# Rows of an edge's destination: from one-hot products against node tiles to a load of 32 nodes by register, and padded weights for 32 experts

## The chip, the cores and the metric

The kernel runs on one core of a Trainium2 chip. The metric is the device time of one execution in microseconds (us); three runs of the kernel before gave 5314.71, 5327.92 and 5352.43, so its median is 5327.92. The engines' names are those of the profile: PE (TensorE), DVE (VectorE), ACT (ScalarE), POOL (GpSimd), SP (SyncE, which issues DMAs here). PEld is PE's loading of weights, that is of the operand that stays in the array during a product.

## The reference

The program is a graph network of four layers, each followed by a mixture of experts. There are 3125 nodes with 256 features, and 50,000 edges with a source, a destination, 64 attributes and a weight; edges are sorted by destination. Cut to what the change touches:

```
# layer 1, messages                       row = source, col = destination
edge_in = concat([h[row], h[col], edge_attr])
msg = relu(edge_in @ W1.T + b1) @ W2.T + b2
agg = segment_sum(msg, row)               # then a GRU cell on agg and h

# layer 1, experts: 32 of 256 -> 64 -> 256, each node goes to its best one
idx = argmax(x @ router_w.T + router_b)
out = relu(relu(x @ W1[idx] + b1[idx]) @ W2[idx] + b2[idx])

# layer 2, hyperbolic convolution         c = 1
x_src, x_dst = x[src], x[dst]
msg = logmap(x_src, x_dst, c)             # needs x_src . x_dst, |x_src|^2, |x_dst|^2
```

The weighted messages of layer 2 are then summed by destination, and a mixture of 8 experts with products of 256 x 512 to 512 x 256 follows. Layer 0 is graph attention with 8 experts, layer 3 two more convolutions with 16 experts.

## The kernel before, in words

Nodes lie in 25 tiles of 128 (the last is padded), edges in 392 tiles of 128 (padded with edges to a node that is none), worked in 28 groups of `GF = 14` edge tiles. Since edges are sorted by destination, the destinations of one edge tile fall into few node tiles. `WIN[i]` lists those that tile `i` may hit, with four standard deviations to spare: 552 pairs in all, 1.41 per edge tile. At the start `windows()` (L684) tests on the chip that the data keeps within them, and a flag chooses between the branch told of here and a general one.

**Rows of the destination.** Layers 1 and 2 need, for every edge, a row that belongs to its destination: in layer 1 the product of the destination's features with a part of W1 (`q`), in layer 2 the features with their square (257 columns). Both are had by a product with a one-hot matrix. `dst_hot` (L352) loads a group's destinations as an int32 row broadcast to 128 partitions (`w_row`, 128 x 1792), and for each node tile that the group may hit it compares them with the node numbers of the partitions (`w_hot`, bf16, on DVE). To keep float32's precision, the rows are split into three bf16 parts that add up (`split3`, or by hand in layer 1). One edge tile then takes three bf16 products for each of its node tiles: 552 x 3 = 1656 products in each layer. `dst_hot` also serves the attention layer.

**Layer 1, first loop** (`mpnn_buckets`, L1169; "MQ" below). `prepare` works on up to four node tiles at a time (seven times): it collects the results of the experts before, normalises, transposes, and takes the product with W1's part; the three parts stay in SBUF (`q_parts`, name `mq_q`). It is called from the loop over groups when a group two further on needs its nodes. For each edge tile PE adds the product of 64 attributes with W1's last part (f32, in two matmul instructions) and the one-hot products in PSUM (`mq_pe`); ACT copies two tiles at a time to `mq_r` (three buffers of a group); POOL scatters every tile's rows by an indirect DMA (L570) into `slot_r`, sorted by the source. A second loop ("mb") takes the sums and the GRU from there.

**32 experts** (`moe_top1`, L1285, by `sparse_experts`, L583). Nodes are sorted into chunks of 128 of the same expert (43 chunks always, more if needed). For a chunk, `load(i)` reads the expert's weights by a register (`se_w`, 4 buffers, 128 x 385 f32) and the chunk's rows (`se_r`), which PE transposes. Products: hidden (128 rows, 64 columns of weights), ACT's relu into `se_h`, to the output (65 rows: 64 hidden ones and a row of ones for the bias, which a DVE memset sets). Loads run two chunks ahead. The rows go back by POOL's indirect DMA.

**Layer 2** (`hyper_bn`, L1537; "HB" below). For each group POOL gathers the sources' rows (`hb_r`), the one-hot matrices are made, and the node tiles that come into reach are split into parts (`hb_parts`, 4 buffers). For each edge tile PE takes the rows of the destinations (`hb_pc`), DVE multiplies and sums them with the sources' rows and copies the squares; then a chain of small operations on the group gives a factor for each edge (`hbe_` names); and with one group's delay, `sums` makes a weighted one-hot matrix (`hb_eq`, DVE) and adds up the messages by destination (`hb_acc`, f32). After every step `between()` lets a piece of other work in: chains of node work, and the products of the mixture for blocks of four node tiles that are complete, at a pace of 0.44 pieces for each call (`PACE`). The weights of these products come through SP (`hb_w`).

The order on every engine is that of the program. SP issues in order the loads of `w_row`, `mq_ea`, `se_w`, `se_r`, `hb_w` and the stores.

The lines that follow are `between`, which sets the order of the work in HB:

```
def between():
    slot[0] += 1
    step(chains)
    if products and slot[0] * PACE >= done[0] + 1:
        done[0] += 1
        step(products)
```

## Time and profile before

The profiled execution took 5317.6 us; its span is 5315.8 us, and the mean granted clock of PE 0.848 of full speed. Busy time over the span: PE 4261.4 us (80%), PEld 2837.0, DVE 2560.1 (48%), POOL 2243.8 (42%), ACT 1177.9 (22%).

| stage | from, to (us) | PE busy | DVE busy | POOL busy | clock | DMA share |
|---|---|---|---|---|---|---|
| attention and windows | 0 to 78 | 36.9 | 51.5 | 14.3 | 0.90 | 0.48 |
| GAT | 78 to 605 | 374.3 | 366.2 | 396.4 | 0.82 | 0.64 |
| 8 experts | 740 to 867 | 117.5 | 100.4 | 66.3 | 0.98 | 0.77 |
| layer 1, first loop (MQ) | 865 to 1456 | 538.4 | 117.6 | 396.7 | 0.89 | 0.52 |
| layer 1, second loop, GRU | 1458 to 2130 | 627.5 | 356.5 | 0 | 0.99 | 0.28 |
| 32 experts | 2130 to 2409 | 162.9 | 128.9 | 66.0 | 0.53 | 0.34 |
| layer 2 (HB) | 2409 to 3705 | 1151.7 | 840.9 | 386.1 | 0.92 | 0.32 |
| layer 3, convolutions | 3709 to 4848 | 896.3 | 368.6 | 748.3 | 0.80 | 0.32 |
| 16 experts | 4860 to 5315 | 313.2 | 167.3 | 120.1 | 0.79 | 0.47 |

"Busy" is the time in which the engine executes; issuing a DMA and the handling of registers are not in it. The clock is the share of full speed that the throttle granted to PE, as a mean over the stage. In a group of the profile, `out<-in` names the tiles, `128*64 128x256` is the size of the operand that stays and of the one that streams through (partitions x elements), `xN` the number of instructions, and behind the bar stand the busy time in us, the mean of one in ns, and the engine's idle time before the group with what ended most of it.

### The profile page before, as it was taken

How to read it: one execution, taken by the hardware profiler on the slowest of the kernel's cores; microseconds unless marked ns; L12 is line 12 of the kernel's file. 1: busy time of each engine (PE TensorE's matmuls, PEld its weight loads, DVE VectorE, ACT ScalarE, POOL GpSimd, SP SyncE). 2: the span in 40 equal slices, each digit the busy share in tenths (PEclk: the TensorE clock that was granted, in tenths of full speed). 3: DMA queues.
4: the chain of work that ended last, by engine and by line, in shares of the span. 5: the costliest groups of instructions: out<-in, count | busy, mean ns of one | idle time of the engine just before them, and what ended most of it. 6: DMA issues, size and time to landing. Idle time of an engine off the chain costs nothing. (4 is left out here: it accounts for less than half of the span.)

```text
span 5315.8 us, 59675 instructions
## 1 busy us (share of the span) xinstructions
PE 4261.4 (80%) x19370; PEld 2837.0 (53%) x19370; DVE 2560.1 (48%) x9525; ACT 1177.9 (22%) x2364; POOL 2243.8 (42%) x2372
## 2 busy tenths in 40 slices
PE   4687558999899999485899999988788788885694
PEld 3566446455466666343566666655445344443583
DVE  5676646211055554447766776752333313336224
ACT  2010112222233333012332443453000200002121
POOL 4777454577700000225533333200777447771521
PEclk7888778799999999557999999988898768885797
DMA  6855256455533221154333333213333223330464
GB/s 200 267 160 160 87 187 212 152 170 162 163 105 97 92 90 53 58 161 136 105 105 97 95 111 110 79 44 91 104 105 104 72 77 104 105 104 29 169 215 135
DMA packets 342776, 647.60 MB, mean 122 GB/s; under 512 B 56019, under 2 KB 248630, under 8 KB 338102
## 3 DMA queue, kind: packets, MB, share of 16 engines
q1 hardware_dynamic: 224160, 339.16, 20.5%
q0 software_dynamic: 108480, 298.44, 18.3%
q10 hardware_dynamic: 9814, 6.03, 0.4%
q8 instruction: 163, 2.67, 0.2%
q14 instruction: 159, 1.30, 0.1%
HBM read 512.20 MB, written 131.23 MB: 121 GB/s over the span
## 5 line engine op out<-in xcount | busy, mean ns | idle before, releaser
L253 POOL DMA_INDIRECT hc_wm<-hc_tabc,src_col x784 | 748.3, 954 | 658.5 <-DMA a_L_gnn_c_b_col<-in_L_gnn_c_b_col 311.8
L337 PE MATMUL w_acc<-hc_wm,w_eq 128*128 128x256 f32 x2208 | 750.5, 467 | 203.1 <-DMA hc_wm<-hc_tabc,src_col 138.4
L337 PEld LDWEIGHTS w_acc<-hc_wm,w_eq 128*128 128x128 f32 x2208 | 438.4, 223 | 515.2 <-DVE w_eq L330 235.3
L330 DVE TENSOR_SCALAR w_eq<-iota,dloc,ew 128x128 f32<-128x128 f32 (+1 forms) x784 | 300.1, 385 | 752.8 <-PE w_acc L337 745.5
L253 POOL DMA_INDIRECT hb_r<-hy_x,src_col x392 | 386.1, 985 | 640.9 <-PE hb_acc L1896 390.6
L570 POOL DMA_INDIRECT slot_x<-xn,sl_i x125 | 122.1, 977 | 969.4 <-DMA se_w<-in_L_ffn_lanes 752.4
L570 POOL DMA_INDIRECT slot_r<-mq_r,bk_i x392 | 397.0, 1013 | 196.4 <-issue 89.8
L253 POOL DMA_INDIRECT gw_m<-gat_h,src_col x392 | 404.3, 1031 | 131.9 <-issue 119.2
L1095 PE MATMUL gw_acc<-gw_m,gw_eqt 128*128 128x264 f32 x1104 | 307.3, 438 | 129.1 <-issue 89.7
L1926 PE MATMUL hb_pc<-hb_parts,w_hot 128*128 128x257 bf16 x1656 | 269.3, 294 | 135.4 <-DVE hbe_a L1931 85.6
L1095 PEld LDWEIGHTS gw_acc<-gw_m,gw_eqt 128*128 128x128 f32 x1104 | 232.6, 217 | 190.5 <-issue 94.1
L570 POOL DMA_INDIRECT rows_y<-se_y,se_to x175 | 179.6, 1026 | 350.7 <-DVE se_y L654 186.4
L1220 PE MATMUL mq_pe<-a_L_gnn_W1T_c,mq_ea 64*128 64x256 f32 x784 | 292.6, 456 | 26.7 <-ACT mq_r L1222 13.7
L1896 PE MATMUL hb_acc<-hb_r,hb_eq 128*128 128x257 f32 x1104 | 292.8, 391 | 12.9 <-DVE hb_eq L1891 12.4
L1926 PEld LDWEIGHTS <-w_hot 128*128 128x128 bf16 x1656 | 159.4, 103 | 261.4 <-DVE hbe_a L1931 124.0
L373 PEld LDWEIGHTS <-w_hot 128*128 128x128 bf16 x3312 | 182.9, 99 | 192.9 <-issue 155.6
L373 PE MATMUL mq_pe<-mq_q,w_hot 128*128 128x256 bf16 x1656 | 265.0, 288 | 0.4 <-DVE mq_q L1202 0.4
L1797 ACT ACTIVATE hb_h<-hb_ph,hb_o,hb_s 128x512 f32<-128x512 f32 (+1 forms) x224 | 162.6, 729 | 412.1 <-PE hb_ph L1795 412.0
L1896 PEld LDWEIGHTS hb_acc<-hb_r,hb_eq 128*128 128x128 f32 x1104 | 201.4, 195 | 76.9 <-issue 27.7
L648 PE MATMUL se_py<-se_w,se_h 128*128 128x256 f32 (+1 forms) x886 | 236.3, 412 | 1.3 <-ACT se_h L641 1.2
L639 PE MATMUL se_ph<-se_xT,se_w 128*128 128x256 f32 (+1 forms) x972 | 235.1, 392 | 0.6 <-DVE se_xT L622 0.5
L641 ACT ACTIVATE se_h<-se_ph,se_w 128x256 f32<-128x256 f32 (+1 forms) x243 | 110.1, 454 | 550.3 <-PE se_ph L639 373.8
(524 smaller groups left out, 7279.9 us busy)
## 6 DMA issues: line engine op xcount, KB each, us to landing
w_row<-in_dst_row SPq DMA_DIRECT2D x84, 896.0 KB
mb_r<-slot_r SPq DMA_DIRECT2D x48, 1156.5 KB
se_w<-in_L_ffn_lanes SPq DMA_DIRECT2D x34, 1026.0 KB
hb_w<-in_L_ffn_W SPq DMA_DIRECT2D x112, 256.0 KB
se_r<-slot_x SPq DMA_DIRECT2D x66, 257.0 KB
se_w<-in_L_ffn_lanes SPq DMA_DIRECT2D x32, 513.0 KB
hb_w<-in_L_ffn_Wo SPq DMA_DIRECT2D x56, 256.0 KB
mq_ea<-in_edge_attrT SPq DMA_DIRECT2D x28, 448.0 KB
```

The lines of the kernel that those rows point to most:

```text
L253: nc.gpsimd.indirect_dma_start(out=dst, out_offset=None, in_=table, in_offset=bass.IndirectOffsetOnAxis(ap=idx, axis=0))
L330: V.tensor_scalar(eq[:, :n], iota256[:, :n], dloc[:, i:i + 1], scale[:, u:u + 1], op0=OP.is_equal, op1=OP.mult)
L337: PE.matmul(acc[t][:, :width], eq[:, k * P:(k + 1) * P], m[:, u, :width], start=i == W_FIRST[t], stop=i == W_LAST[t])
L373: PE.matmul(o, hot[t][:, u * P:(u + 1) * P], parts[:, t, k, :width], start=start and j == 0, stop=j == len(ops) - 1)
L570: d = nc.gpsimd.indirect_dma_start(out=table, in_=rows, in_offset=None, out_offset=bass.IndirectOffsetOnAxis(ap=idx, axis=0)).ins
L639: PE.matmul(ph[:fp], w[:, c * f + j * P:c * f + j * P + fp], xT[:, c], start=c == 0, stop=c == 1)
L648: PE.matmul(py[:, u], h[:kp, j, u * P:(u + 1) * P], w[:kp, o2 + j * D:o2 + (j + 1) * D], start=j == 0, stop=j == nj - 1)
L1095: PE.matmul(acc[t][:, :W], eq[:, k * P:(k + 1) * P], m[:, u], start=False, stop=i == W_LAST[t])
L1220: PE.matmul(pt[:, v], ea[:, (u + v) * P:(u + v + 1) * P], w1c, start=True, stop=False)
L1797: S.activation(o[:, j, :n], ph[:, :n], AF.Relu, bias=shift[i][:, e, j:j + 1], scale=scale[i][:, e, j:j + 1])
L1896: PE.matmul(acc[t][:, :D + 1], eq[:, k * P:(k + 1) * P], b[:, u], start=i == W_FIRST[t], stop=i == W_LAST[t])
L1926: PE.matmul(pc[:, :D + 1], hot[t][:, u * P:(u + 1) * P], parts[t][:, 0, k], start=z == 0, stop=z == len(ops) - 1)
```

## The change

It has three parts.

**Destinations' rows.** In MQ and HB `near_rows` takes the place of `dst_hot` and `from_dst` (the attention layer keeps `dst_hot`). Two neighbouring edge tiles, 256 edges, have destinations within 32 nodes; `windows()` tests this too and writes a table `near_row` of each destination's distance to the first of its pair. The three parts of every node lie in a DRAM table as neighbouring rows (`q_tab`, `parts_tab`), so 32 nodes are 96 rows, which one DMA loads from an address that a register holds (`n_near`, one for each pair of edge tiles, seven in a group). `n_hot` compares the distances (a broadcast row on 96 partitions) with `third`, the number of the partition's node, 0 to 31, each three times. One product of 96 rows for an edge tile gives the sum of the parts: 392 products in each layer.

**Tables.** `prepare` writes the parts to a tile of its own and SP stores it to `q_tab`; in HB `split_to` splits the node tiles in order, up to two groups ahead, and SP stores each to `parts_tab`. `prepare` is called when a group one further on needs its nodes and the 32 rows behind them.

**32 experts.** The weights are laid out as 128 x 2 x 193 and loaded into the end of rows of 257 whose first 64 columns were set to zero once for each of four buffers. Both products are then 128 by 128; the bias of the output comes from a hidden row that is always one, and the memset for each chunk goes.

```diff
+NEAR = 32
+W_TO = [max(WIN[(g + 1) * GF - 1]) + 2 for g in range(ET // GF)]
...
+    def near_rows(pool, g, table, width, bufs=2):
+        row = pool.tile([3 * NEAR, GF * P], BF16, name="n_row")
+        nc.sync.dma_start(row, near_row[g:g + 1].to_broadcast([3 * NEAR, GF * P]))
+        hot = pool.tile([3 * NEAR, GF * P], BF16, name="n_hot")
+        V.tensor_scalar(hot, row, third, None, op0=OP.is_equal)
+        near = pool.tile([3 * NEAR, GF // 2, width], BF16, name="n_near", bufs=bufs)
+        for k in range(GF // 2):
+            i = g * GF + 2 * k
+            with tc.issue_after(near_last[0].ins) if near_last else nullcontext():
+                n = nc.values_load(col["dst"][0:1, i:i + 1], engines=[mybir.EngineType.SP], min_val=0, max_val=N)
+            near_last[:] = [nc.sync.dma_start(near[:, k], table[bass.ds(n * 3, 3 * NEAR)])]
+        return hot, near
...
+                padded = [wp.tile([P, 2, 2 * P + 1], F32, name=f"se_w{k}") for k in range(4 if f < P else 0)]
+                for w in padded:
+                    V.memset(w[:, :, :P - f], 0.0)
...
+                    if f < P:
+                        w = padded[i % 4]
+                        last = nc.sync.dma_start(w[:, :, P - f:],
+                                                 I[name][bass.ds(e * P, P)].rearrange("p (c x) -> p c x", c=2))
...
-                        if f < P:
-                            V.memset(h[f:f + 1], 1.0)
...
-                                PE.matmul(ph[:fp], w[:, c * f + j * P:c * f + j * P + fp], xT[:, c],
-                                          start=c == 0, stop=c == 1)
-                            S.activation(h[:fp, j], ph[:fp], act, bias=w[:fp, o1 + j:o1 + j + 1])
+                                PE.matmul(ph, w[:, c, :P] if f < P else w[:, c * f + j * P:c * f + (j + 1) * P],
+                                          xT[:, c], start=c == 0, stop=c == 1)
+                            bias = w[:, 0, 2 * P:] if f < P else w[:, o1 + j:o1 + j + 1]
+                            S.activation(h[:, j], ph, act, bias=bias)
...
+    near_row = tc.dram_tile([ET // GF, GF * P], BF16, name="near_row")
+    third = const.tile([3 * NEAR, 1], F32, name="third")
...
+        nc.scalar.dma_start(dr, I["dst_row"].rearrange("(a b) -> a b", b=2 * c))
+        V.tensor_copy(rr, dr)
...
+        V.tensor_copy(rb, rr)
+        nc.scalar.dma_start(near_row.rearrange("g (a b) -> (g a) b", b=2 * P), rb.rearrange("n (a b) -> n a b", b=2 * P))
...
-            q_parts = p.tile([P, NT, 3, D], BF16, name="mq_q")
+            q_tab = tc.dram_tile([NR * 3, D], BF16, name="mq_q")
...
-                    o = q_parts[:, t0 + t:t0 + t + m]
+                    o = tp.tile([P, 2, 3, D], BF16, name="mq_o", bufs=2)[:, :m]
...
+                    nc.sync.dma_start(q_tab.rearrange("(t p k) d -> p t k d", p=P, k=3)[:, t0 + t:t0 + t + m], o)
...
-                    ahead = WIN[min((g + 2) * GF, ET) - 1][-1]
-                    while blocks and blocks[0][0] <= ahead * P:
+                    ahead = W_TO[min(g + 1, ET // GF - 1)]
+                    while blocks and blocks[0][0] < ahead * P:
...
-                    hot = dst_hot(ep, g)
+                    hot, near = near_rows(ep, g, q_tab, D, 3)
...
-                            from_dst(pt[:, v], hot, i, q_parts, D, start=False)
+                            PE.matmul(pt[:, v], hot[:, (u + v) * P:(u + v + 1) * P], near[:, u // 2], start=False, stop=True)
...
+            def split_to(end):
+                while split[0] < end:
+                    t = split[0]
+                    split[0] += 1
+                    o = wp.tile([P, 1, 3, D + 1], BF16, name="hb_parts", bufs=2)
+                    split3(sp, o[:, :, :, :D], xn[:, t:t + 1])
+                    split3(sp, o[:, :, :, D:], x2[:, t:t + 1].unsqueeze(2))
+                    nc.sync.dma_start(parts_tab[3 * t * P:3 * (t + 1) * P].rearrange("(p k) d -> p k d", k=3), o[:, 0])
...
-                hot = dst_hot(ep, g, 1)
-                for t in sorted(hot):
-                    if t not in parts:
-                        parts[t] = wp.tile([P, 1, 3, D + 1], BF16, name="hb_parts", bufs=4)
...
+                split_to(min(NT, W_TO[min(g + 2, ET // GF) - 1]))
+                hot, near = near_rows(ep, g, parts_tab, D + 1, 3)
...
-                    ops = [(t, k) for t in WIN[i] for k in range(3)]
-                    for z, (t, k) in enumerate(ops):
-                        PE.matmul(pc[:, :D + 1], hot[t][:, u * P:(u + 1) * P], parts[t][:, 0, k],
-                                  start=z == 0, stop=z == len(ops) - 1)
+                    PE.matmul(pc[:, :D + 1], hot[:, u * P:(u + 1) * P], near[:, u // 2], start=True, stop=True)
```

## The prediction

> **What bounds the kernel now.** I read the page's 40 slices first, one slice being 133 us:
>
> ```profile
> PE   4687558999899999485899999988788788885694
> DVE  5676646211055554447766776752333313336224
> POOL 4777454577700000225533333200777447771521
> PEclk7888778799999999557999999988898768885797
> ```
>
> No one engine carries the span. The change touches three stretches: the first loop of the message layer ("MQ", 865 to 1456 us, slices 7 to 11), the 32 experts (2244 to 2370, slices 17 and 18, clock 5) and the hyperbolic layer ("HB", 2409 to 3705, slices 19 to 28). The groups name their work:
>
> ```profile
> L570 POOL DMA_INDIRECT slot_r<-mq_r,bk_i x392 | 397.0, 1013 | 196.4 <-issue 89.8
> L1926 PE MATMUL hb_pc<-hb_parts,w_hot 128*128 128x257 bf16 x1656 | 269.3, 294 | 135.4 <-DVE hbe_a L1931 85.6
> L1220 PE MATMUL mq_pe<-a_L_gnn_W1T_c,mq_ea 64*128 64x256 f32 x784 | 292.6, 456 | 26.7 <-ACT mq_r L1222 13.7
> L373 PE MATMUL mq_pe<-mq_q,w_hot 128*128 128x256 bf16 x1656 | 265.0, 288 | 0.4 <-DVE mq_q L1202 0.4
> ```
>
> The change takes 1264 of each 1656 bf16 products away. What that is worth depends on who ends last in each stretch. In MQ it is POOL, by its waits between 893 and 1456:
>
> ```profile
> POOL slot_r L570 <- issue: 89.8, 295, 0.3
> POOL slot_r L570 <- ACT mq_r L1222: 53.9, 30, 10.3
> POOL slot_r L570 <- DMA slot_r<-mq_r,bk_i: 20.4, 62, 1.8
> ```
>
> A scatter is 0.97 us of work and 0.30 of issue, so 392 take 500 us at best; the stretch takes 562. PE's answers (mq_r) cost 53.9 of the difference. So a faster PE can win at most some 54 us here. The stretches say where:
>
> ```profile
> 984.00:1036.00 52.00, 51.98 (x150) 23.24 (x150) 4.90 (x12) 7.88 (x14) 30.10 (x31) 0.50 0.38 125
> 1059.00:1105.00 46.00, 46.00 (x249) 24.81 (x248) 5.21 (x7) 10.55 (x18) 35.50 (x35) 1.00 0.59 191
> 2310.00:2330.00 20.00, 20.00 (x60) 11.11 (x60) 8.86 (x29) 2.53 (x7) 6.79 (x7) 0.50 0.52 162
> 2460.00:2510.00 50.00, 37.95 (x204) 24.47 (x202) 43.70 (x268) 7.22 (x12) 38.42 (x39) 0.86 0.46 138
> 2700.00:3460.00 760.00, 719.08 (x3233) 481.08 (x3233) 526.91 (x2868) 293.88 (x550) 235.28 (x238) 0.97 0.32 99
> ```
>
> (Columns: length, busy PE, weight loads, DVE, ACT, POOL, granted clock, DMA share, GB/s.) PE is busy without a gap in the first three, yet at clock 0.50 in two of them. Rows 4 and 5: HB's start is DVE's (43.7 of 50), its long middle PE's (719 of 760).
>
> **MQ, part by part.** PE's timeline prices one edge tile:
>
> ```profile
> 1027.08 1.46 PE L373 MATMUL mq_pe<-mq_q,w_hot 128*128 128x256 bf16 x6
> 1028.47 1.22 PE L1220 MATMUL mq_pe<-a_L_gnn_W1T_c,mq_ea 64*128 64x256 f32 x2
> 1181.02 0.70 PE L1220 MATMUL mq_pe<-a_L_gnn_W1T_c,mq_ea 64*128 64x256 f32 x2
> 1181.65 0.50 PE L373 MATMUL mq_pe<-mq_q,w_hot 128*128 128x256 bf16 x3
> ```
>
> From start to start, at clock 1.0 the f32 pair takes 0.63 us and three bf16 products 0.43 (six: 0.76), so one is 0.43 − 2 × 0.11 = 0.21 and a tile after the change 0.84. At 0.50 the pair takes 1.15, six take 1.39, three 0.76, so one 0.32: a tile 1.47. POOL's pace is 1.275. **The clock therefore decides the sign:** at 1.0 POOL stays the bound and nearly all of the 54 is won; at 0.50 PE becomes the bound.
>
> What grants the clock? I weighed each product by streamed columns times rows over 128 and read the clock from one 3.4 us stretch to the next over the whole trace. From 1.0 it fell in every stretch under 600 columns per us, in 40 of 50 between 600 and 840, in 2 of 33 at 960 to 1080, and never above. From 0.50 it never rose under 720, rose in 26 of 74 between 840 and 960, and nearly always above 1020. Before the change a tile is 1024 × 64/128 + 4.22 × 256 = 1592, over 1.275 us 1250 per us: it holds. After it, 512 + 256 × 96/128 = 704: 552 per us at POOL's pace, 838 back to back at 1.0, 479 at 0.50. So the clock falls and stays down, except around the seven `prepare` blocks, whose 128-row f32 products lift it for some 10 us each.
>
> [...]
>
> Sum of MQ: 392 × 1.47 = 576; PE's share of `prepare` 57 (busy PE of 524 without the tiles' time); bursts at 1.0 save 7 × 8 tiles × 0.63 = 35. New on the path is what follows each `prepare`: the parts no longer stay in SBUF but go through SP to a DRAM table, and the next rows wait for that store. That is a copy chain, a store and a load of some 2.5 us each (transfers that size here), with 15 to 30 PE instructions between in the program's order: 3 to 4 us shown, seven times, 25. Together 623 against 562: **+60**. Bounds: −45 (clock kept, stores hidden), +110 (no bursts, 8 us at each block).
>
> SP: a load by register costs about 1.13 us (four expert weights in 3.74 us), so seven per group take 8 of the group's 18 us in MQ and of 40 in HB. Covered; bounds 0 to +60, the latter in the third rival. The row broadcast shrinks (896 KB of int32 over 128 partitions to 344 KB); the DMA share of 0.5 leaves that without effect.
>
> **HB.** In the middle there are 257 edge tiles in 760 us, 2.96 each. hb_pc holds PE 173.7 us for 1101 there, 0.158 each; 4.28 per tile become one, so PE gives back 3.28 × 0.158 = 0.52 of 2.96 us. Next late is DVE: 526.9/257 = 2.05 busy per tile, less a little (40 w_hot of 0.82 us become 18 n_hot). PE's 2.44 remains above it, but DVE already waits for PE's answers (hb_pc 74 us, hb_acc 59) and the two hand work back and forth, so I count 0.35, not 0.52: 257 × 0.35 = 90. The start (2460 to 2610) is DVE's; there the clock will fall (1448 + 193 columns per tile in 2.1 us is 780 per us), and PE at 0.50 needs 1.5 us of DVE's 2.0: nothing, −15 to +20. The last 245 us hold products alone and stay. Splitting the parts moves earlier and through SP; its DVE and ACT work is the same. **HB −90**, bounds −135 (all of 0.52) and −35 (a quarter, if DVE's chain sets the pace).
>
> **Experts.** A chunk takes 2.765 us with PE full at 0.50. Padding to 128 raises the weighted work from 512 + 1024 + 520 = 2056 to 512 + 1024 + 1024 = 2560, from 744 to 924 columns per us, into the band where the clock rose in a third of the stretches; with 35 stretches it should rise, and then hold (2560 per 1.95 us is 1310). PE would need 1.4; next late are the weights: four buffers, the next load issued when a chunk's last product frees one, then two issues (0.84) and a landing near 2 us inside 1.5 chunks, so 1.9 to 2.0 per chunk. 43 × 0.8 = 34: **−33**; without the flip 0 to +5 (64 more columns of weights to load, beside matmuls). The 43 memsets go (0.17 us, off the path).
>
> **The rest.** `windows` gains a load, ten small DVE operations and a store at the kernel's start; the first group of each layer now waits for split, store and load in series. By such latencies here (2.5 us each) +12, bounds +5 and +25.
>
> Sum: 60 − 90 − 33 + 12 = −51, from 5317.6 (span 5315.8 and 1.8 outside; the median shown, 5327.9, lies 0.2% above): **5267 us**.
>
> **Rivals.** (1) *The clock holds in MQ.* For: `prepare` lifts it, back to back 838 is only just short. Against: 552 at POOL's pace. −40 − 100 − 33 + 12: 5157. (2) *DVE takes over HB's middle.* For: 526.9 of 760 busy and 85.6 us of PE idle before hb_pc on hbe_a. Against: DVE's own waits for PE sum to 170 us. +60 − 35 − 33 + 12: 5322. (3) *Rows come late,* the slower side: one SP queue carries stores, register loads and HB's product weights in order, a store waits for the near loads issued before it, and the rows for the store. It decides where PE is the bound and reaches a group within the 8 us of its seven loads. Seven blocks of MQ at 8 us instead of 3.5 and half of HB's 28 groups at 5 us: +31 + 70 over the forecast, and no bursts at full clock, +35: 5403. Against: in HB's middle rows are issued 140 PE instructions ahead.
>
> **Numbers.** This kernel's measurement tells about 1% from no change. Forecast 0.42 (its own range 5217 to 5317: MQ and HB 25 either way each), rival (1) 0.14, (2) 0.26, (3) 0.18. Faster by over 1% (under 5264): half of the forecast, (1) and a little of (2), 0.38. Within: the other half and most of (2), 0.37. Slower: (3) and some of (2), 0.25. Range: (1)'s time to (3)'s, cut by a tenth on each side, 5150 to 5400.
>
> **What would show it.** Right: MQ at clock 0.5 to 0.7 with PE full, tiles of 1.47 us, POOL waiting for mq_r; the experts at 1.0 and 2 us a chunk; HB's middle 2.6 us per tile. Wrong: a clock of 1.0 in MQ (the weighing by rows fails), PE idle on n_near (rows late), or HB's tile pace unchanged with DVE full.

## The result

The changed kernel takes 5330.69 us (median of 12 runs, 5302.06 to 5338.44), the kernel before in the same comparison 5327.58 (12 runs, 5308.93 to 5352.43). The ratio is 0.9995, 95% interval 0.9975 to 1.0016: no change that can be measured, where 5267 us had been forecast. The profiled execution after took 5330.3 us, 12.7 more than the one before. The stages did move, against each other:

| from, to | before (us) | after (us) | difference | forecast |
|---|---|---|---|---|
| start to MQ's first scatter | 893.9 | 900.6 | +6.7 | |
| MQ, first to last scatter | 561.4 | 652.8 | +91.4 | +60 |
| second loop, GRU, to the experts' first product | 792.4 | 793.1 | +0.6 | |
| 32 experts, to the last rows out | 123.1 | 92.5 | -30.6 | -33 |
| to HB's first edge tile | 63.5 | 69.3 | +5.7 | |
| HB's edge tiles | 1033.3 | 972.2 | -61.1 | -90 |
| rest | 1848.0 | 1848.0 | 0.0 | |

The three lines without a forecast of their own were one term together, +12, and came to +13.0. (The times of the table are starts of instructions in the two traces, for the last rows out the end; HB's edge tiles are counted from the first to the last on DVE.)

Ten of the runs below fell in times in which every kernel, the one before too, took 15 to 17 per cent longer, with gaps of some 9 us in several engines at once that no instruction explains (the kernel before took 6153 to 6221 us there), so runs over 6000 us are compared among themselves, and the main readings rest on the others.

The 40 slices after, 133 us each, as the page has them:

```profile
PE   4787558889889999842788999888888788775694
DVE  5776645110115545535867776652333313336224
POOL 4777454556540000032733423200777447771521
PEclk7888777555569999966799899888788668985797
```

Slices 8 to 11, MQ, now stand at clock 5, where a 7 and three 9s stood. The groups that answer to those of before:

```profile
L590 POOL DMA_INDIRECT slot_r<-mq_r,bk_i x392 | 382.3, 975 | 307.2 <-ACT mq_r L1275 199.4
L1273 PE MATMUL mq_pe<-a_L_gnn_W1T_c,mq_ea 64*128 64x256 f32 x784 | 451.5, 689 | 13.8 <-DMA mq_ea<-in_edge_attrT 13.8
L1985 PE MATMUL hb_pc<-n_near,n_hot 96*128 96x257 bf16 x392 | 120.3, 314 | 178.5 <-DVE hbe_a L1989 102.9
```

POOL now waits 199 us for mq_r, PE's answer, where it waited 53.9. The edge product, which nobody touched, has gone from 292.6 us of PE to 451.5: same instructions, lower clock. Stretch by stage (columns as above: length, busy PE, weight loads, DVE, ACT, POOL, clock, DMA share, GB/s):

```profile
893.00:1555.00 662.00, 588.07 (x1298) 265.68 (x1298) 70.25 (x197) 134.54 (x235) 382.33 (x392) 0.53 0.47 140
2350.00:2430.00 80.00, 60.65 (x308) 40.15 (x306) 37.57 (x112) 14.06 (x39) 37.71 (x39) 0.98 0.73 215
2700.00:3480.00 780.00, 716.86 (x2626) 457.56 (x2626) 525.45 (x2952) 312.91 (x581) 248.10 (x259) 0.92 0.36 101
```

MQ has a mean clock of 0.53, the experts 0.98, HB's middle 0.92 (0.97 before). And PE's timeline in MQ (start, length, instruction):

```profile
967.07 1.22 PE L1273 MATMUL mq_pe<-a_L_gnn_W1T_c,mq_ea 64*128 64x256 f32 x2
968.23 0.39 PE L1274 MATMUL mq_pe<-n_near,n_hot 96*128 96x256 bf16 x1
968.55 1.22 PE L1273 MATMUL mq_pe<-a_L_gnn_W1T_c,mq_ea 64*128 64x256 f32 x2
```

From 967.07 to 968.55 is one edge tile: 1.48 us, where 1.47 had been worked out.

### The profile page after: what moved, and what is told of

Read it like the earlier page. It is cut to its first block, busy times and chain, and to the rows that moved or that the text cites. A ratio compares the mean times of both kernels' runs of the same rounds, so it can differ in the third digit from the quotient of the medians.

```text
span 5328.5 us, 57042 instructions
## 1 busy us (share of the span) xinstructions
PE 4180.3 (78%) x16842; PEld 2718.5 (51%) x16842; DVE 2479.0 (47%) x9433; ACT 1182.0 (22%) x2364; POOL 2219.5 (42%) x2373
## 5 line engine op out<-in xcount | busy, mean ns | idle before, releaser
L590 POOL DMA_INDIRECT slot_r<-mq_r,bk_i x392 | 382.3, 975 | 307.2 <-ACT mq_r L1275 199.4
L1273 PE MATMUL mq_pe<-a_L_gnn_W1T_c,mq_ea 64*128 64x256 f32 x784 | 451.5, 689 | 13.8 <-DMA mq_ea<-in_edge_attrT 13.8
L1961 PE MATMUL hb_acc<-hb_r,hb_eq 128*128 128x257 f32 x1104 | 310.3, 413 | 19.3 <-DVE hb_eq L1956 13.0
L1961 PEld LDWEIGHTS hb_acc<-hb_r,hb_eq 128*128 128x128 f32 x1104 | 216.7, 208 | 110.1 <-issue 40.1
L1273 PEld LDWEIGHTS mq_pe<-a_L_gnn_W1T_c,mq_ea 64*128 64x128 f32 x784 | 200.1, 307 | 135.4 <-issue 126.8
L1985 PE MATMUL hb_pc<-n_near,n_hot 96*128 96x257 bf16 x392 | 120.3, 314 | 178.5 <-DVE hbe_a L1989 102.9
L667 PE MATMUL se_ph<-se_xT,se_w 128*128 128x256 f32 (+1 forms) x972 | 219.1, 370 | 3.2 <-DMA se_w<-in_L_ffn_lanes 0.8
L1333 PE MATMUL mb_acc<-mb_m,mb_eq 128*128 128x264 f32 x880 | 215.2, 390 | 0.3
L676 PE MATMUL se_py<-se_w,se_h 128*128 128x256 f32 x886 | 212.8, 383 | 2.9 <-ACT se_h L670 2.7
L1275 ACT COPY mq_r<-mq_pe 128x512 f32<-128x512 f32 x196 | 115.0, 587 | 446.1 <-PE mq_pe L1274 437.0
```

Of the source, the lines that this page charges most:

```text
L590: d = nc.gpsimd.indirect_dma_start(out=table, in_=rows, in_offset=None, out_offset=bass.IndirectOffsetOnAxis(ap=idx, axis=0)).ins
L667: PE.matmul(ph, w[:, c, :P] if f < P else w[:, c * f + j * P:c * f + (j + 1) * P], xT[:, c], start=c == 0, stop=c == 1)
L676: PE.matmul(py[:, u], h[:, j, u * P:(u + 1) * P], w[:, :, P:2 * P] if f < P else w[:, o2 + j * D:o2 + (j + 1) * D], start=j == 0, stop=j = ...
L1273: PE.matmul(pt[:, v], ea[:, (u + v) * P:(u + v + 1) * P], w1c, start=True, stop=False)
L1333: PE.matmul(acc[:, :W], eq[:, k], f[:, k], start=k0 + k == 0, stop=k0 + k == B_TILES[b] - 1)
L1961: PE.matmul(acc[t][:, :D + 1], eq[:, k * P:(k + 1) * P], b[:, u], start=i == W_FIRST[t], stop=i == W_LAST[t])
```

## The experiments

### 128 rows in MQ: what the narrow products cost

```diff
-            w1c = load_t(p, "L1_gnn_W1T_c")
+            w1c = p.tile([P, D], F32, name="mq_w1c")
+            V.memset(w1c[64:], 0.0)
+            nc.scalar.dma_start(w1c[:64], I["L1_gnn_W1T_c"])
+            eas = [p.tile([P, GF * P], F32, name=f"mq_ea{k}") for k in range(2)]
+            for ea in eas:
+                V.memset(ea[64:], 0.0)
...
-                    ea = ep.tile([64, GF * P], F32, name="mq_ea")
-                    nc.sync.dma_start(ea, I["edge_attrT"][:, g * GF * P:(g + 1) * GF * P])
-                    hot, near = near_rows(ep, g, q_tab, D, 3)
+                    ea = eas[g % 2]
+                    nc.sync.dma_start(ea[:64], I["edge_attrT"][:, g * GF * P:(g + 1) * GF * P])
+                    hot, near = near_rows(ep, g, q_tab, D, 3, P)      # 128 rows
```

> The changed kernel, with both products of an edge tile in MQ widened from 64 and 96 rows to 128: the rows added hold zeros in the edge attributes and no match in the one-hot matrix, so the sum is the same, and PE streams exactly as many columns. Theory (the clock goes by columns weighted with rows): a tile weighs 1280 instead of 704, that is 871 per us back to back at clock 0.50, where it rose in about a third of the stretches, and 1004 at POOL's pace, where it almost never fell; so MQ runs at 1.0, POOL is the bound again, MQ takes 520 to 560 us instead of 660 and the kernel 5190 to 5235. Rival 1 (the clock goes by how long PE is busy, or by streamed columns alone): nothing changes, 5330. Rival 2 (rows come late through SP, and that holds MQ): the loads grow by a third, so 5330 to 5350, with PE waiting for n_near.

It took 6063 us beside 6156 for the kernel before (0.9865, 0.9787 to 0.9943). A second run:

> Again the changed kernel with both products of an edge tile in MQ widened to 128 rows of which the added ones hold zeros: the first time it ran on a chip where the kernel before took 6156 us, all engines standing still for some 9 us now and then. There MQ's products took 316 us of PE in place of 579, and a tile's f32 pair 0.43 us instead of 0.63 at clock 1.0, so widening does two things: it lifts the clock, and a product of 128 rows lets the next weights load beside it. Where the kernel before takes 5328: theory (PE at half clock with its loads uncovered holds MQ) 5190 to 5240, with MQ at 1.0 in most stretches (1280 weighted columns per 1.275 us, 1004 per us) and 520 to 560 us long. Rival (rows late, or anything else than PE's own pace): 5310 or more.

6081 beside 6153 (0.9883, 0.9861 to 0.9904). MQ took 645 and 644 us in these two. A third run:

> A third time the changed kernel with both products of an edge tile in MQ at 128 rows, since the two chips before were slowed by long gaps in all engines (the kernel before took 6155 us there). Where the kernel before takes about 5328: theory (PE at half clock with uncovered loads of weights holds MQ) 5190 to 5240, MQ 520 to 560 us at a clock above 0.9. Rival (rows late): 5310 or more. On a slowed chip: as before, some 1.2 per cent under the kernel before.

5261.98 us, 5327.10 before (0.9870, 0.9834 to 0.9906), and so 69 us under the changed kernel's median. MQ takes 579 us (653). That is most of what had been lost, though short of the 520 to 560 expected. PE's timeline at clock 1.0, and MQ as a whole:

```profile
1061.60 0.60 PE L1278 MATMUL mq_pe<-mq_w1c,mq_ea 128*128 128x256 f32 x2
1062.03 0.27 PE L1279 MATMUL mq_pe<-n_near,n_hot 128*128 128x256 bf16 x1
1062.14 0.60 PE L1278 MATMUL mq_pe<-mq_w1c,mq_ea 128*128 128x256 f32 x2
```

```profile
893.00:1490.00 597.00, 287.81 (x1322) 207.09 (x1322) 78.16 (x225) 137.21 (x242) 381.06 (x391) 0.74 0.54 167
```

A tile now takes 0.54 us from start to start (1061.60 to 1062.14), where at this clock 0.84 had been worked out for 64 and 96 rows; at 0.50 the trace has 1.067 where it had 1.475. The same columns stream through. PE is busy for 288 us in place of 588. The clock, though, is 0.74 and not above 0.9 as the theory had it: PE now works in bursts and is idle for 309 of the 597 us, and in the trace of the kernel before the clock fell after each of the 36 stretches at 1.0 that had under 600 weighted columns per us. So with 128 rows two things changed, MQ's mean clock (0.53 to 0.74) and the length of a tile at either clock, and the next run looks at each. By these prices either would be enough to bring PE under POOL's 1.275 us: 0.84 with 64 rows at 1.0, 1.067 with 128 rows at 0.50.

### 96 rows

```diff
-            w1c = p.tile([P, D], F32, name="mq_w1c")
-            eas = [p.tile([P, GF * P], F32, name=f"mq_ea{k}") for k in range(2)]
+            w1c = p.tile([3 * NEAR, D], F32, name="mq_w1c")
+            eas = [p.tile([3 * NEAR, GF * P], F32, name=f"mq_ea{k}") for k in range(2)]
...
-                    hot, near = near_rows(ep, g, q_tab, D, 3, P)
+                    hot, near = near_rows(ep, g, q_tab, D, 3)
```

(The diff is against the run before.)

> The changed kernel, with the edge product in MQ widened to 96 rows only, as many as the product of the near rows has. It tells the two effects of widening apart. If weights load beside products again as soon as both have 96 rows, a tile costs 1.07 us at clock 0.50 and 0.54 at 1.0, and POOL's 1.275 is the bound at either clock. Theory (the clock goes by columns weighted with rows): 1024 x 96/128 + 192 = 960 columns per tile, 753 per us at POOL's pace, where it fell in three quarters of the stretches, so MQ's clock stays at 0.5 to 0.7 though a tile is cheap, and the kernel takes 5200 to 5250. Rival 1 (the clock goes by busy time or plain columns): the same clock as with 128 rows. Rival 2 (only 128 rows let the weights load): tiles of 1.47 us at 0.50, MQ 650 us, 5330.

6062 us beside 6153 (0.9853, 0.9835 to 0.9872), MQ 644.5 us, as long as with 128 rows (645 and 644). What the run has to tell stands in PE's timeline:

```profile
1415.96 0.60 PE L1278 MATMUL mq_pe<-mq_w1c,mq_ea 96*128 96x256 f32 x2
1416.40 0.27 PE L1279 MATMUL mq_pe<-n_near,n_hot 96*128 96x256 bf16 x1
1416.51 0.60 PE L1278 MATMUL mq_pe<-mq_w1c,mq_ea 96*128 96x256 f32 x2
```

0.55 us per tile at 1.0, 1.067 at 0.50: as with 128 rows, so rival 2 falls. In the changed kernel, at 0.50, the two f32 products of a tile take 0.588 and 0.563 us from start to start, and 0.427 where all products have 96 or 128 rows. Yet it is not the 64 rows by themselves that cost. Where the trace of the changed kernel has several edge products in a row, one between two others takes 0.427 us too (0.216 at clock 1.0):

```profile
1077.57 2.07 PE L1273 MATMUL mq_pe<-a_L_gnn_W1T_c,mq_ea 64*128 64x256 f32 x4
1079.58 0.39 PE L1274 MATMUL mq_pe<-n_near,n_hot 96*128 96x256 bf16 x1
```

These four start 0.588, 0.427, 0.426 and 0.564 us apart. The price stands where products of 64 rows and products of 96 or 128 take turns (with 128, in MQ before, 0.588 and 0.563 us too), and most tiles of MQ have such a turn. At the 669 turns of MQ after, and the 763 of MQ before, where the next product came within 0.8 us, its load of weights started at most 5 ns ahead of it (1079.575 us, the product at 1079.579); between equal rows it started at least 106 ns ahead, beside the product before (1078.164, that product at 1078.162). An order with more edge products in a row would have fewer turns; no run tried it.

For the clock: in the traces before and after it is 1.0 or 0.50, and within the span each value lasts a whole number of stretches of 3.413 us. Those in MQ that were at 0.50 and held edge tiles alone can be sorted by the share of PE's cycles in which columns streamed, and by rows. (At 0.50 a bf16 product of 256 columns takes 0.213 us among its like, so a stretch has room for some 4100 columns; those of an f32 product, 0.427 us, count twice. All are counted to the stretch in which their product starts.)

| edge and near rows | columns in 0.8 to 0.9 of cycles: rose to 1.0 | 0.9 and more: rose |
|---|---|---|
| 64 and 96 (changed kernel) | 0 of 36 | 0 of 4 |
| 64 and 128 (before) | 4 of 18 | |
| 96 and 96 | 0 of 8 | 21 of 29 |
| 128 and 128 (five runs) | 7 of 10 | 82 of 82 |

At the same share of streaming cycles the clock rose the oftener the more rows were in use. Rival 1 (busy time or plain columns) would have equal shares in each column of the table, and falls. Some of the groups are small, and their counts shift by some when the columns are spread over the product's time; the order of the rows stays. MQ's mean clock hardly differs between 96 and 128 rows (435 of 645 us at 0.50, and 390), and in both PE stands idle between bursts (with 128 rows it was busy for 316 of 640 us).

### How MQ's loss divides: rows earlier, prepare earlier or later, more buffers

Rival (3) of the prediction was that rows come late. The first edit calls `prepare` two groups ahead.

```diff
-                    ahead = W_TO[min(g + 1, ET // GF - 1)]
+                    ahead = W_TO[min(g + 2, ET // GF - 1)]
```

> The changed kernel, with prepare in MQ called two groups ahead instead of one, as far ahead as before the change; stores and loads of the rows then have a group more of cover. Rival (rows come late): most of the 96 us that MQ lost comes back, 5235 to 5270. Theory (PE at half clock is the bound, and the waits for n_near are 26 us of it): at most those 26 us, 5300 to 5330, with MQ's clock still near 0.53 and tiles of 1.45 us.

6072 us beside 6156 (0.9887, 0.9808 to 0.9965), MQ 652 us, with the clock at 0.52 and 578 us of PE: it tells that PE was the bound there too, and not more. The second loads everything of a group one group earlier, ahead of the stores of the next block:

```diff
                 for g in range(ET // GF):
-                    ahead = W_TO[min(g + 1, ET // GF - 1)]
-                    while blocks and blocks[0][0] < ahead * P:
-                        prepare(*blocks.pop(0))
-                    ea = ep.tile([64, GF * P], F32, name="mq_ea")
...
+                    ea, hot, near = following
+                    if g + 1 < ET // GF:
+                        following = loads(g + 1)
+                    upto(g + 2)                   # prepare what W_TO[g + 2] needs
```

> The changed kernel with the loads of a group in MQ issued one group earlier, ahead of prepare, and its products left at 64 and 96 rows. If PE's 1.475 us per tile at clock 0.50 is the larger part of MQ's loss of 91 us (392 tiles x 0.2 us above POOL's pace, 78 us) and late rows the smaller: MQ 600 to 640, the kernel 5280 to 5315. If late rows are the larger part: MQ 540 to 580, the kernel 5220 to 5255. If prepare's own chain makes the gaps: 5325 to 5335.

5335.55 us, 5328.79 before (1.0000, 0.9966 to 1.0035): the third case of the expectation, MQ 659 us. Where PE needed 1.475 us for a tile, 578 for all, earlier rows won nothing. With 128 rows as well:

> The changed kernel with both products of an edge tile in MQ at 128 rows, and with the loads of a group (edge attributes, distances, near rows) issued one group earlier, ahead of the prepare that the group after it needs, so that they wait for no store of that block. With 128 rows alone MQ took 579 us of the 515 that POOL's pace allows; six gaps in the scatters, 77 us, stood at prepare. Theory now (rows that wait behind prepare's stores are the rest of MQ's loss): most of the 77 us go, MQ 515 to 540, the kernel 5200 to 5225. Rival (the gaps are prepare's own chain of gather, norm and product, whatever the rows wait for): MQ 570 to 580, the kernel 5255 to 5265.

5256.88, 5328.79 before (0.9861, 0.9783 to 0.9939); MQ 574 us, five less than with 128 rows alone. The rival is right: late loads of rows are not what is left. Then `prepare` behind the products of a group:

```diff
-                    upto(g + 2)
                     r = ep.tile([P, GF, D + 1], F32, name="mq_r", bufs=3)
...
+                    upto(g + 2)
```

> The kernel of the run with 128 rows and loads one group earlier, with prepare called after the products of a group instead of ahead of them. In that run DVE stood 381 us in MQ before the copy into mq_r, for a buffer that POOL's scatters had to free, and prepare's DVE work came behind it in order; four gaps of 18 us were left in the scatters. Theory (prepare's own chain of some 50 us starts only when DVE is past that wait, with two groups, 36 us, left for POOL; after the products it has three, 54 us): the gaps go, MQ 520 to 540 instead of 574, the kernel 5200 to 5225. Rival (the gaps come from the rows or from the clock, not from this order): MQ 570 to 580, 5250 to 5265.

5268.50, 5337.47 before (0.9866, 0.9815 to 0.9918); MQ 576 us. The gaps stayed, and so did the wait that the theory was built on (DVE's waits in MQ of this run):

```profile
DVE mq_r L1281 <- DMA slot_r<-mq_r,bk_i: 380.3, 24, 20.1
```

Last, five buffers for mq_r instead of three, with 128 rows and with the products as changed:

```diff
-                    r = ep.tile([P, GF, D + 1], F32, name="mq_r", bufs=3)
+                    r = ep.tile([P, GF, D + 1], F32, name="mq_r", bufs=5)
```

> The changed kernel with both products of an edge tile in MQ at 128 rows, as in the first of these runs, and five buffers of a group for mq_r instead of three (SBUF has room, since the parts no longer lie there). Moving prepare behind a group's products left its gaps (73 us in four) where they were. DVE stands some 17 us per group before its copy into mq_r, until POOL has scattered the group that held the buffer, and in the gap at 1148 us prepare's DVE work stood behind two such waits. Theory (three buffers tie DVE, and with it prepare, to POOL's pace): with five, DVE and PE run two groups further ahead, 36 us, more than the longest gap of 27; the gaps go, MQ 515 to 540 instead of 579, the kernel 5200 to 5225. Rival (the chain through SP's queue and the tables is too long for any ring): MQ 570 to 580, 5255 to 5270.

> The changed kernel with five buffers of a group for mq_r in MQ instead of three, and its products left at 64 and 96 rows. If PE is MQ's bound at 1.475 us per tile (578 us for 392, and prepare's own PE work of some 50 us), five buffers win only what the gaps at prepare added, 10 to 30 us: MQ 620 to 645, the kernel 5300 to 5325. If the gaps at prepare are the larger part of MQ's 91 us: MQ under 600, the kernel under 5280.

6131 and 6143 us beside 6221 (0.9862, 0.9824 to 0.9900; 0.9860, 0.9826 to 0.9894). MQ took 646 us with 128 rows (644 and 645 with three buffers) and 665 with the narrow products. The gaps in the scatters stood at the same edge tiles, and were as long, as with three buffers: after tiles 153, 209 and 279 they were 26.3, 12.2 and 23.9 us, in the run of 5262 us with three buffers 26.8, 12.3 and 23.8.

Neither edit took DVE's wait away, so neither tests the theory. With five buffers and 128 rows DVE still waited 314 us for mq_r (370 with three, in the first run with 128 rows). DVE's timeline at the gap after tile 153, the last of group 10, first with three buffers (5262 us), then with five:

```profile
1122.09 0.18 DVE L1273 COPY mq_r<-sloc 128x14 f32<-128x14 f32 x1 [15.53 <-DMA slot_r<-mq_r,bk_i]
1126.75 1.38 DVE L210 TENSOR_SCALAR xn<-x,ln_mv,ln_rs 128x256 f32<-128x256 f32 x4
```

```profile
1363.85 0.18 DVE L1273 COPY mq_r<-sloc 128x14 f32<-128x14 f32 x1 [15.48 <-DMA slot_r<-mq_r,bk_i]
1368.51 1.38 DVE L210 TENSOR_SCALAR xn<-x,ln_mv,ln_rs 128x256 f32<-128x256 f32 x4
```

The copy is DVE's first write to a group's mq_r. Counted through the trace, it is that of group 13 with three buffers and that of group 15 with five: the first write to a buffer that group 10 held, which POOL has just emptied. `prepare`'s normalising (xn) stands behind it in DVE's order, so it starts only when POOL has nothing left, and PE's next edge tile comes 18 us after xn (from 1126.75 to 1144.85, in the first of the two). With more buffers the copy only moved further ahead in DVE's order. So the engines' order is not that of the source. In the kernel before, DVE wrote the last xn of all seven calls at 984.5 us, when POOL had begun 64 of its 392 scatters; in the run of 5262 us, with the table, two calls come after scatter 154 and two after scatter 280, where the two longest gaps are. That this order makes them is read from the traces; no edit moved the copy.

### MQ as before, the rest as changed

```diff
     def mpnn_buckets(pos, slot_r, collect, weights):
-            q_tab = tc.dram_tile([NR * 3, D], BF16, name="mq_q")
+            q_parts = p.tile([P, NT, 3, D], BF16, name="mq_q")
...
-                    hot, near = near_rows(ep, g, q_tab, D, 3)
+                    hot = dst_hot(ep, g)
```

> The changed kernel with MQ alone as it was before (dst_hot, from_dst, parts in SBUF); HB, the experts and the test of the 32 nodes stay changed. If the stages' sums hold by themselves (MQ +96, HB -61, experts -31, the rest +9), MQ takes 562 again and the kernel 5235, 1.7 per cent less than before the change. If part of what HB and the experts gained was only a shift of what MQ had done (stores, memory traffic, state of the clock), more than 5260.

> Again the changed kernel with MQ alone as it was before, since its first run fell on the slow chip. If the stages' sums hold by themselves (MQ +96, HB -61, experts -31, the rest +9): 5235. If part of what HB and the experts gained was only moved there from MQ: over 5260.

6045 beside 6156 (0.9865, 0.9780 to 0.9950) and 6091 beside 6153 (0.9907, 0.9876 to 0.9938), with MQ at 645 and 652 us. Whether the stages add up to 5235, these two don't tell. The same with the edge product widened to 128 rows:

> The kernel of the run before this, and the edge product of MQ as it was before the change widened from 64 to 128 rows, the added ones zero. Theory (clock by weighted columns): a tile weighs 1024 + 1080 = 2104 instead of 1592, the 50 us at clock 0.50 near 1000 us go or shrink, and the f32 pair drops from 0.63 to 0.43 at clock 1.0, so PE (0.43 + 0.46) keeps below POOL's 1.275: MQ 520 to 540 instead of 562 and the kernel 5195 to 5220. Rival (MQ before was POOL's and the clock only follows from waits elsewhere): 5235, as without the widening.

6031 beside 6153 (0.9792, 0.9765 to 0.9819), MQ 599 us, 46 to 53 less than without the widening. And a second run:

> Again, on another chip: the changed kernel with MQ as before the change, and its edge product widened from 64 to 128 rows with zeros. Where the kernel before takes about 5328: if the stages add up, 5235 without the widening; with it a tile costs 0.76 to 1.09 us of PE at clock 1.0 instead of 1.06 to 1.39 (as on the slowed chip), so MQ comes near POOL's pace, 520 to 540 us instead of 562, and the kernel 5195 to 5220. Rival (what HB and the experts gained was moved there from MQ, or MQ's rest is not PE's): 5235 or more.

5215.76, 5337.47 before (0.9766, 0.9714 to 0.9818): **the fastest of all the kernels here**, 2.3 per cent under the one before. MQ takes 541 us, HB 969, so HB keeps its gain without MQ's change, and the rival falls. MQ of this kernel, POOL's waits and the stretch:

```profile
POOL slot_r L590 <- issue: 96.2, 316, 0.3
POOL slot_r L590 <- ACT mq_r L1279: 61.8, 26, 31.4
POOL slot_r L590 <- DMA slot_r<-mq_r,bk_i: 12.8, 42, 0.3
```

```profile
893.00:1450.00 557.00, 400.12 (x2587) 314.28 (x2587) 104.75 (x254) 134.46 (x243) 398.16 (x392) 0.86 0.54 169
```

Now MQ's 653 us can be taken apart. From the changed kernel to 128 rows it falls by 73 (to 579): the narrow products at half clock. From there to this kernel, which differs from it in the way the destinations' rows come, by 38 (to 541): the table in DRAM, with its store and loads and with `prepare` late in DVE's order, against parts in SBUF. Gaps over 3 us between scatters sum to 77 us with the table and 23 without, and the three longest named above, 63 us together, have no like without it. The kernel before lies 20 above this one, from which it differs in MQ by its 64 rows alone.

### HB: is it DVE or PE?

```diff
-                    V.tensor_copy(a2[:, u:u + 1], pc[:, D:D + 1])
...
+                V.memset(a2, 0.25)
```

> The changed kernel, with one DVE operation per edge tile left out in HB: the copy of the destination's square (0.15 us, 392 times, 59 us of DVE), in whose place one constant stands for the group, so the output isn't the reference's. Rival (DVE's work took over as HB's bound and ate the missing 30 us): most of the 59 us comes off, 5270 to 5285. Theory (PE stays the bound in HB's middle, and the half clock there, 110 us more of it than before, ate the gain): only the start, where DVE is the bound, gets shorter, 8 of 28 groups or some 15 us, and some waits of PE for DVE, 5300 to 5320.

> Again the changed kernel without the copy of the destination's square in HB (0.15 us of DVE, 392 times, 59 us; a constant stands in its place, so the output isn't the reference's); its first run fell on a slowed chip, where HB gained 11 us by it. Where the kernel before takes about 5328: rival (DVE took over as HB's bound and ate the missing 30 us) 5270 to 5285; theory (PE and its clock set the middle, DVE only the start) 5300 to 5320.

6046 beside 6156 (0.9843, 0.9765 to 0.9920) the first time, and 5505.06 the second, where the kernel before took 5328.79 (1.0338, 1.0252 to 1.0425): **174 us over the changed kernel, with less to do**. HB took 1146 us (972). DVE's waits in HB name it:

```profile
DVE hbe_den L1997 <- DMA hb_r<-hy_x,src_col: 182.5, 22, 11.0
```

hbe_den multiplies the squares of destination and source. With the copies gone, only the gathers were left ahead of it, and it stands up to 91 us ahead of the group's last edge tile on DVE (0.6 to 1.5 us behind it in the changed kernel). So DVE stood 182.5 us for gathers, with everything behind it. The run says nothing on the load of DVE. The next one keeps the order and moves the copy to ACT:

```diff
-                    V.tensor_copy(a2[:, u:u + 1], pc[:, D:D + 1])
+                    S.copy(a2[:, u:u + 1], pc[:, D:D + 1])
```

> The changed kernel, with the copy of the destination's square in HB made by ACT instead of DVE (392 times 0.15 us, 59 us off DVE; the order of the steps stays). The run that left the copy out moved a later DVE operation ahead of it in DVE's order, which then waited for gathers, so it told nothing of DVE's load. Rival (DVE took over as HB's bound): HB 930 instead of 972 us, the kernel 5285 to 5300. Theory (PE with its clock bounds the middle): HB 950 to 975, 5305 to 5335. It gets slower, over 5340, if ACT, where the copy stands in order behind the waits for the mixture's products, answers PE later than DVE did.

5348.52, 5337.47 before (1.0006, 0.9978 to 1.0035). HB took 968 us, where in six runs with HB as changed it took 967 to 972: 59 us off DVE moved nothing. DVE's load is not the bound. What the run doesn't test is the handing back to PE, for PE waits for this copy before it writes hb_pc again, whichever engine makes it (PE's waits in HB's middle, after and in this run; 25.2 us before the change):

```profile
PE hb_pc L1985 <- DVE hbe_a L1989: 44.6, 56, 5.3
PE hb_pc L1985 <- ACT hbe_a L1989: 50.4, 47, 4.9
```

Then PE:

```diff
-                    PE.matmul(pc[:, :D + 1], hot[:, u * P:(u + 1) * P], near[:, u // 2], start=True, stop=True)
+                    for _ in range(3):
+                        PE.matmul(pc[:, :D + 1], hot[:, u * P:(u + 1) * P], near[:, u // 2], start=True, stop=True)
```

> The changed kernel, with the product of the destinations' rows in HB issued three times over (each overwrites the one before, the result is the same), 0.23 us of PE per edge tile more at clock 1.0, as before the change in PE's load and all else as after. Rival 1 (DVE bounds HB): no change, 5325 to 5340. Rival 2 (PE alone bounds it and the clock has no part): some 340 tiles x 0.23 us = 78 us, 5400 to 5410. Theory (PE bounds it, and the half clock is fed by what PE left out): two thirds of that is given back by stretches at clock 1.0, 110 us of half clock fall to about 80, and the kernel takes 5350 to 5380.

5384.07, 5337.47 before (1.0087, 1.0053 to 1.0120): 49 us above the changed kernel when each is taken against its own runs of before (1.0087 − 0.9995, of 5330), near the upper end of the theory, and under rival 2's 70 to 80, though the two intervals leave some 28 to 70. HB took 1009 us, 37 more, where six traces with HB as changed lie within 6 us of one another. By groups 9 to 27, HB's middle and end, with the time at clock 0.50 read from the trace:

| | time (us) | of it at 0.50 | if that half were at 1.0 |
|---|---|---|---|
| before | 785.3 | 51.2 | 759.7 |
| after | 734.3 | 129.7 | 669.5 |
| three products | 762.4 | 102.4 | 711.2 |

The last column takes half of the time at 0.50 off; it is an estimate, as if PE alone set the pace there. By it the change won 90 us, and 39 of them went to the lower clock. The six traces with HB as changed have 109 to 130 us at 0.50, so 29 to 39. The threefold product cost 42 by that column and 28 in time; its 102 us at 0.50 lie just under those six. Its added products are worth 61 us (266 tiles, two of 0.114 us each), so part of them fell into PE's idle time. That more work on PE costs time in HB, where less on DVE wins none, is shown; how much the clock took back is worked out, and no edit isolates it.

## Why the prediction was wrong

It forecast -51 us, and the profiles have +12.7. Of the difference of 64, 31 lie in MQ and 29 in HB.

**MQ, +60 forecast, +91.4.** That the clock decides the sign was right: the tile of 1.47 at 0.50 came as 1.475, PE became the bound, and POOL waits 199.4 us for mq_r. The mean clock was 0.53 while PE was busy for 588 of 662 us.

Between the first and the last scatter PE spent 543 us on edge tiles, 38 on `prepare`'s products, and stood idle for 72; the sum had 576 − 35 = 541, 57 and 25. **The failed step is the 25 for what follows each `prepare`.** It counted the copies, the store and the rows behind `prepare`'s products, and put what those products themselves wait for at nothing. PE's waits in MQ after:

```profile
PE bt_p L995 <- DVE xn L210: 37.3, 5, 9.8
PE mq_pe L1274 <- DMA n_near<-mq_q: 25.7, 4, 8.1
PE mq_pe L1274 <- DVE n_hot L385: 5.2, 1, 5.2
```

The rows make 31 us of it, and the larger part, 37, is PE waiting for `prepare`'s normalised tiles, which stand behind a wait for POOL in DVE's order, as above. Nor are there seven such places: three calls come within the first three groups, the other four in two pairs. Why the order came out so is open.

**"Bursts at 1.0 save 7 × 8 tiles × 0.63 = 35" failed too**, without showing in the sum. The clock still rose at `prepare`, seven times for 3.4 or 6.8 us, but PE then stood and waited, and the clock had fallen again before the tiles came: of some 330 edge tiles that lie wholly in one clock, three ran at 1.0. The 28 edge products that ran at 1.0 saved 8 us. That the tiles still came to 543 is luck: 78 edge products in a row with others took 0.427 us and saved 12, and 12 were made before the first scatter.

A cause was missed as well. The prediction put 0.11 us per run of bf16 products down as a fixed part, and took the pair's 0.63 as the price of its columns. Both hold loads of weights in the open, at the turns between the edge product's 64 rows and 128: with 128 rows throughout the pair took 0.43 and the bf16 product 0.11. One reading is off without weight: the range given is the two rivals' times rounded, with nothing cut off them.

**HB, -90 forecast, -61.1.** The size of the gain in PE's work was right: 90 us at full clock over groups 9 to 27, by the estimate above. **The failed step is that its price was taken at a clock of 1.0 in the middle and the fall was looked for only at the start.** With work taken off PE the weighted columns fell there too, from 2030 per us (2700 to 3460 us before) to 1865 (2700 to 3480 after), and the time at 0.50 in groups 9 to 27 went from 51 to 130 us (109 to 130 over six traces). By the same estimate that took 39 of the 90 back, and groups 0 to 8, counted at nothing, gave 10: 61. The reason given for counting 0.35 us a tile and not 0.52 (the handing back and forth with DVE) is not settled: taking 59 us off DVE changed nothing, but PE's waits for the copy rose from 25.2 to 44.6 us in HB's middle. At 1.0 a product took 0.114 us from start to start and not the 0.158 of the busy time, and 3.28 x 0.114 is 0.37, so the 0.35 comes out without that reason.

**The experts, -33 forecast, -30.6.** Right, by its own steps but one: the clock rose to 0.98, and a chunk takes 2.02 us (median from one output product to the next chunk's), just over the 1.9 to 2.0. Late next were to be the weights; PE waited 15.0 us for the rows (se_r) and 0.8 for the weights. How much of it is the clock and how much the 65-row product's loads (before, at 0.50, its two halves took 0.585 and 0.564 us from start to start, where 128 rows took 0.427) no run parts.

**The rest, +12, came as 13.0.** MQ's first scatter comes 6.7 us later, and the way from the experts to HB's first edge tile is 5.7 us longer.

**The rivals.** (1), the clock holds, came nowhere near: no run shows its −40 for MQ, which came to +91.4 at a mean clock of 0.53. (2) gave 5322, close to what was measured, but DVE's load does not bound HB, as the copy on ACT shows. (3), rows late, has a part in MQ, where PE waited 25.7 us for rows, and 38 us go with the table at `prepare`; issuing the loads earlier brought back 5, so SP's queue as the cause isn't shown. In HB's middle PE's waits name no n_near. The chance for "within 1 per cent" was 0.37; it is what came.

## What to carry to other kernels

Before products are made fewer or narrower, look at what that does to the engine's clock and to its loads of weights: here, at 0.50, an edge tile whose 64 rows took turns with 96 cost 1.475 us of PE, and one with 128 rows, zeros among them, 1.067; and with less to do PE ran MQ at a mean clock of 0.53 where it had had 0.90. A gain on one engine is to be priced at the clock that is left when the work is gone, not at the one in the profile (in HB 39 of 90 us went that way, by the estimate above). And a wait that an experiment takes away, or a buffer that it adds, can let an operation move up in its engine's order, where it blocks all behind it, as hbe_den did for 182.5 us: look at the order before the time is read.

## What the hardware showed that was not expected

- Where f32 products of 64 rows took turns with bf16 products of 96 (MQ after) or 128 (MQ before), weights were not loaded beside the product ahead: at clock 1.0, before, the two halves of the pair took 0.32 and 0.31 us from start to next against 0.216, and at 0.50, in both, 0.588 and 0.563 against 0.427. The bf16 product between them paid too, 0.325 at 0.50 in MQ after against 0.213 for as many columns among its like in MQ before. Among others of 64 rows the f32 product took the 0.427 and 0.216 as well. A turn between 96 and 128 rows showed no such price: in HB after, at 1.0, 0.216 us ahead of a 96-row product and 0.114 behind it.
- The granted clock went with the rows in use: of MQ's stretches at 0.50 with 0.8 to 0.9 of PE's cycles streaming, 0 of 36 rose with 64 and 96 rows, 7 of 10 with 128. The weighing put forward in the prediction, columns times rows over 128, sorted the stretches of the changed kernel too, from which it was not made: from 1.0 the clock fell after every stretch under 720 columns per us (58), after 43 of 70 between 720 and 960, after 1 of 32 between 960 and 1080 and after none above (760); from 0.50 it rose after 1 of 506 under 840.
